# A two-layer image model on one Trainium2 core: zero rows written behind the upsampled filters, constants loaded beside the upsampling, an own order for image 0's first pass, and the convolution's input ahead of the scan constants

## The chip, the cores and the metric

The kernel runs as one program on one core of a Trainium2 chip. The core has a matrix engine (TensorE, PE in the profile; its weight loads are the row PEld), a vector engine (DVE), an activation engine (ACT), a general engine (POOL) and SyncE (SP), which here issues every DMA of the program. Each engine runs its own instructions in order and waits for the others on semaphores. The metric is the device time of one execution in microseconds. Before the change it is 26376.83 us, the median of three runs (26376.42 to 26384.82).

## The reference, cut to what matters

The input is `x`, eight images of 128x128 pixels with 96 channels, float32. There are two layers. Each adds a mixer to its input and then a small feed-forward net whose numbers are rounded to 8-bit floats.

```python
# layer 0
x_pre = soa(einsum('bhwc,mc->bhwm', ln(x), w1))     # soa(x) = scale * relu(x)**2 + bias
xf = rfft2(x_pre)                                   # 128 x 65 frequencies, 192 channels
filts = [Rh @ cw @ Rw for cw in (cw0, cw1, cw2)]    # three small filters, upsampled to 128 x 65
gctx = ln(x).mean((1, 2)); sctx = relu(bn(ln(x) @ sp_w.T)).mean((1, 2))
r = softmax((soa([gctx, sctx] @ fc1.T) @ fc2.T).reshape(b, 3, 192), 1)
x = x + irfft2(xf * (filts * r).sum(0)) @ w2.T
x = x + ffn(ln(x))
# layer 1
xi, z = split(ln(x) @ W_in.T)
u = silu(depthwise_conv3x3(xi) + conv_b)            # zero padded
y = scan(u, forward) + scan(u, backward)            # state-space recurrence over the 16384 pixels
x = x + (y * silu(z)) @ W_out.T
x = x + ffn(ln(x))
```

The weights of an image's filters (`r`) depend on means over the whole image, so an image's first pass over its pixels has to end before its filter stage starts.

## The kernel before

`tile_metaformer_kernel` (L1679 on) sets up tensors in device memory and runs four parts one after the other.

**Zero rows.** `xcd` holds the convolution's input of all images with padding rows above and below each. L1691 to L1700 clear a tile `z` on DVE and write it with 32 DMAs (L1697 one row, L1698 nine rows, each for 128 and for 64 channels of eight images), 960 KB for an image.

**Upsampling** (`upsample_filters`, L253 to L283). The small filters are loaded into a tile `cw` that DVE clears first (L261), by three DMAs (L265). 64 groups of three channels follow: 18 matrix products (L274), one ACT copy out of PSUM into one of three buffers `upt` (L282), and one DMA of 146 KB to `tall` (L283). Four PSUM tiles go round. Then its pools are closed.

**Layer 0** (`layer0`, L286). First come 21 constant loads (most in `load`, L306, with one SP issue each), then a schedule written out by hand: each step of a group of four image rows has a time in a table, a `Plan` sorts all steps by their times, and that order is the order on the engines. The times set an order only; when an instruction runs is settled by its waits. `first_steps` is an image's first pass: 32 groups, each with a load `ax` (L359), a normalisation (L92 to L115 on DVE, ACT and POOL), four transposes on PE (L364), an ACT copy `axnt` that also sums (L370), the context product (L376 on PE, L380 on ACT), two projections of two rows each (L389 on PE, relu L402 and square L409 on ACT, scaling into `img` L416 on DVE) and a POOL copy of the sums (L428). Then `gate_steps` works out the weights `r`, and `filter_steps` runs over the 64 channel groups, `token_steps` over the 32 pixel groups. The first pass of image 1 lies beside the token steps of image 0, and so on; the first pass of image 0 has nothing beside it. It is scheduled with the table `ALONE`, which is `LAST` with other times for `keep`, and with a period of 6.0 in that table's units (L882).

**Layer 1** (`scan_layer`, L902). At its start the feed-forward constants are loaded through a pool `scf`, which is closed before the work pool `scw` is opened in the same place. Then all other constants are loaded, from L934 to L998: 53 DMAs, with the DVE and ACT work on them. After that a second `Plan` runs: convolution chunks (`conv_steps`: load `xin` L1019, nine products per half chunk against diagonal matrices `cdiag` L1035, ACT eviction `pre` L1049, silu L1060, store `ud` L1067), preparation (`prepare_steps`) and the scans (`scan_steps`), which take four fifths of the time.

Outside the hand-written plans the framework orders instructions by their dependencies and the order in the text. SP's DMAs carry eight semaphores in turn: a DMA is issued only when the eighth before it has landed.

Of the kernel before, what the change touches and what calls it, by code (L numbers as in the profile page):

```python
# [9 lines left out]
F32 = mybir.dt.float32  # L10
# [242 lines left out]
def upsample_filters(tc, p, tall):  # L253

    nc = tc.nc
    with ExitStack() as ctx:
        one = ctx.enter_context(tc.tile_pool(name="up1", bufs=1))
        two = ctx.enter_context(tc.tile_pool(name="up2", bufs=3))
        psum = ctx.enter_context(tc.tile_pool(name="upp", bufs=4, space=PSUM))
        cw = one.tile([96, 32, M * 2], F32, name="cw")  # L260
        nc.vector.memset(cw, 0.0)  # L261
        rw = one.tile([96, KW], F32, name="rw")
        nc.sync.dma_start(rw, p.rwt)
        for s, src in enumerate((p.cw0, p.cw1, p.cw2)):
            nc.sync.dma_start(cw[32 * s : 32 * s + CWW[s], 0 : CWH[s], :], src)  # L265
        cwv = cw.rearrange("p h (m c) -> p h m c", c=2)
        G = 3
        for g in range(M // G):
            ps = psum.tile([96, G, 2, KW], F32, tag="up", name="up")
            for i in range(G):  # L270
                for c in range(2):
                    for s in range(NS):
                        q = slice(32 * s, 32 * s + CWW[s])
                        nc.tensor.matmul(  # L274
                            ps[32 * s : 32 * s + 32, i, c, :],
                            cwv[q, :, g * G + i, c],
                            rw[q, :],
                            start=True,
                            stop=True,
                        )  # L280
            t = two.tile([96, G, 2 * KW], F32, tag="upt", name="upt")
            nc.scalar.copy(t, ps.rearrange("p g c k -> p g (c k)"))  # L282
            nc.sync.dma_start(tall[:, g * G : (g + 1) * G, :], t)  # L283


def layer0(tc, p, tall, x2d, xcd, zsd):  # L286

    nc = tc.nc
    with ExitStack() as ctx:
        cp = ctx.enter_context(tc.tile_pool(name="l0c", bufs=1))  # L290
        gp = ctx.enter_context(tc.tile_pool(name="l0g", bufs=1))
        psum = ctx.enter_context(tc.tile_pool(name="l0p", bufs=8, space=PSUM))
# [49 lines left out]

        wk = ctx.enter_context(tc.tile_pool(name="l0w", bufs=2))

# [488 lines left out]
        ALONE = {**LAST, "keep": (-3.4, -5.3)}  # L833
# [47 lines left out]
        with tc.manual_schedule():  # L881
            at = first(0, 0.0, 6.0, ALONE, ALONE, ALONE)  # L882
            for b in range(B):
                steps = filter_steps(wk, FILTER)
                plan.pipeline(at, range(M // 3), 3.6, lambda g: steps)
                at += (M // 3 - 1) * 3.6 + 16.6
                if b < B - 1:
                    begin = first(b + 1, at, 11.6, FIRST, NEXT, LAST)
                tsteps = token_steps(b, wk, TOKEN)
                plan.pipeline(at, range(NTG), 11.6, lambda g: tsteps)  # L890
                at = begin
            plan.emit()
# [9 lines left out]
def scan_layer(tc, p, x2d, xcd, zsd, ud, yfd, dld, bcd, out):  # L902
# [11 lines left out]
    with ExitStack() as ctx:  # L914
# [8 lines left out]
        with tc.tile_pool(name="scf", bufs=1) as lp:  # L923
            ffn = Ffn(nc, cp, lp, "f1", p.f1_w1t, p.f1_b1, p.f1_w2t, p.f1_b2, ident8, mhalf)
        wk = ctx.enter_context(tc.tile_pool(name="scw", bufs=2))
        w1 = ctx.enter_context(tc.tile_pool(name="sc1", bufs=1))
        psa = ctx.enter_context(tc.tile_pool(name="scpa", bufs=2, space=PSUM))
        ps1 = ctx.enter_context(tc.tile_pool(name="scp1", bufs=1, space=PSUM))

        wo = cp.tile([128, 3, 2, C + 1], F32, name="wo")  # L930
        nc.vector.memset(wo, 0.0)
        for h in range(2):
            q = slice(64 * h, 64 * h + 64)
            nc.sync.dma_start(wo[q, :, h, 0:C], p.woutt.rearrange("(n d) c -> d n c", d=64))  # L934
            nc.vector.reduce_sum(
                wo[q, :, h, C : C + 1], wo[q, :, h, 0:C], axis=mybir.AxisListType.X
            )

        selx = cp.tile([128, 4, 128], F32, name="selx")
        nc.sync.dma_start(selx, p.selx)  # L940
        sely = cp.tile([128, 32], F32, name="sely")
        nc.sync.dma_start(sely, p.sely)

# [7 lines left out]
        dtb = cp.tile([128, 2, 2], F32, name="dtb")  # L951
        for k, parts in enumerate(kinds):
            for q, c in parts:
                nc.sync.dma_start(cwt[q, k, :], p.conv_w[c, :])
                nc.sync.dma_start(cbt[q, k : k + 1], col(p.conv_b, c.start, c.stop))
                for d in range(2):
                    lo, hi = d * M + c.start, d * M + c.stop
                    nc.sync.dma_start(dtb[q, d, k : k + 1], col(p.dt_b, lo, hi))
        at = cp.tile([128, 2, NB, NG], F32, name="at")
        nc.sync.dma_start(at, p.a_logs)  # L960
        nc.scalar.activation(at, at, AF.Exp)
        nc.vector.tensor_scalar(at, at, -1.0, None, ALU.mult)
        cdiag = cp.tile([128, 2, 9, 128], F32, name="cdiag")

        ddiag = cp.tile([128, 3, 128], F32, name="ddiag")
        dsk = cp.tile([128, 2, 3], F32, name="dsk")
        for h in range(2):
            for d in range(2):
                nc.sync.dma_start(
                    dsk[64 * h : 64 * h + 64, d, :],  # L970
                    p.ds[d * M : (d + 1) * M].rearrange("(n c) -> c n", c=64),
                )
        dsum = cp.tile([128, 3], F32, name="dsum")
        nc.vector.tensor_tensor(dsum, dsk[:, 0, :], dsk[:, 1, :], ALU.add)
        for n in range(3):
            nc.vector.tensor_scalar(ddiag[:, n, :], ident, dsum[:, n : n + 1], None, ALU.mult)
        for k in range(2):
            for j in range(9):
                nc.vector.tensor_scalar(
                    cdiag[:, k, j, :], ident, cwt[:, k, j : j + 1], None, ALU.mult  # L980
                )

        NX = 4 * NST + 2 * NR
        xpw = cp.tile([128, 2, 3, NX], F32, name="xpw")
        nc.vector.memset(xpw, 0.0)
        dtw = cp.tile([NX, 2, 3, 128], F32, name="dtw")
        nc.vector.memset(dtw, 0.0)
        for d in range(2):
            for t in range(3):
                for q, b, c in tile_parts(0, t):  # L990
                    for lo, n, at0 in (
                        (NR, NST, b * NST),
                        (NR + NST, NST, 2 * NST + b * NST),
                        (0, NR, 4 * NST + b * NR),
                    ):
                        nc.sync.dma_start(xpw[q, d, t, at0 : at0 + n], p.xpt[d, c, lo : lo + n])
                    lo = 4 * NST + b * NR
                    nc.sync.dma_start(dtw[lo : lo + NR, d, t, q], p.dtt[d, :, c])  # L998
# [653 lines left out]
        with tc.manual_schedule():  # L1652
            plan = Plan()
            plan(-300, lambda: nc.vector.memset(h0, 0.0))
            for bp in range(B // 2):
# [23 lines left out]
def kernel(ctx: ExitStack, tc: tile.TileContext, p: Params, out: bass.AP):  # L1679
# [11 lines left out]
    with tc.tile_pool(name="zero", bufs=1) as zp:  # L1691
        z = zp.tile([128, (HB + 1) * W], F32, name="z")
        nc.vector.memset(z, 0.0)
        for b in range(B):
            for c in (slice(0, 128), slice(128, M)):
                n = c.stop - c.start
                nc.sync.dma_start(xcd[b, c, 0, :], z[:n, 0:W])  # L1697
                nc.sync.dma_start(  # L1698
                    xcd[b, c, H + 1 : XROWS, :], z[:n, :].rearrange("p (h w) -> p h w", w=W)
                )  # L1700

    upsample_filters(tc, p, tall)
# [111 lines left out]
```

## Time and profile before

The profiled execution took 26377.52 us, of which the span from the first to the last instruction is 26375.7 us. Stage borders below are from the instructions in order of time.

| stage | from us | to us | what ends it |
|---|---|---|---|
| zero rows, first loads | 0.0 | 29.3 | SP issues the upsampling's first load |
| clear and load `cw` | 29.3 | 53.9 | third slice of `cw` landed |
| upsampling on PE | 53.9 | 137.3 | last L274 product |
| constants of layer 0, first `ax` | 137.3 | 152.1 | first L92 of image 0 |
| image 0, first pass | 152.1 | 373.9 | last context sum (L380) |
| its weights | 373.9 | 385.0 | first L528 of the filter stage |
| rest of layer 0 | 385.0 | 5146.0 | last ACT step of the last token group |
| constants of layer 1 | 5146.0 | 5182.9 | first L1035 |
| convolution ahead of the scans | 5182.9 | 5323.6 | first L1252 |
| scans | 5323.6 | 26375.7 | end |

| engine | busy us | share of the span |
|---|---|---|
| PE | 22322.2 | 85% |
| DVE | 25019.3 | 95% |
| ACT | 17618.2 | 67% |
| POOL | 22505.7 | 85% |

A row of instructions gives its start in us after the span's start, its length, the engine, the line, what it writes and reads, how many were merged, and in brackets how long the engine was idle before it and who ended that. "SPq" rows are DMA issues: the time is that of the issue, not of the transfer.

### The profile page before, as it was taken

Reading aid. Unit: us, or ns where it says so; the run is one execution under the profiler, and the core shown is the slowest. Engines: PE = TensorE matmul, PEld = TensorE weight load, DVE = VectorE, ACT = ScalarE, POOL = GpSimd, SP = SyncE. Lnnn points to the kernel's source line nnn. Section 1 sums busy time; section 2 is a strip of 40 time slices with the busy share of each in tenths; the row PEclk is TensorE's granted clock in tenths of the full one; section 3 lists DMA queues with packets and bytes.
Section 4 is the critical chain, followed back from the end, with each engine's and each line's share of the span. In section 5 each row is a group of like instructions: output and inputs, shape, how many; then the busy total and the mean of one; then the engine's idle time right before and its main releaser. Section 6 shows DMA issues by size and latency. Waiting matters only on the chain.

```text
span 26375.7 us, 272252 instructions
## 1 busy us (share of the span) xinstructions
PE 22322.2 (85%) x84560; PEld 8957.9 (34%) x84560; DVE 25019.3 (95%) x18514; ACT 17618.2 (67%) x31776; POOL 22505.7 (85%) x13815
## 2 busy tenths in 40 slices
PE   8999999889997777899977778998777788877777
PEld 6777777622222222222222222222222222212222
DVE  5888888699999999999999999999999999999999
ACT  5888887556666666666666666666666666656666
POOL 3666666489999999999999999999999999999998
PEclk9999999999998888999988889999888899988888
DMA  2333333344444444444444444444444444444443
GB/s 61 94 94 95 94 92 89 86 154 154 155 159 136 136 136 139 148 158 156 155 139 135 138 135 155 154 153 154 140 137 137 136 151 155 153 144 135 135 139 114
DMA packets 1887106, 3513.56 MB, mean 133 GB/s; under 512 B 564382, under 2 KB 999190, under 8 KB 1885626
## 3 DMA queue, kind: packets, MB, share of 16 engines
q1 hardware_dynamic: 1885652, 3496.14, 41.7%
q8 instruction: 672, 11.01, 0.2%
q14 instruction: 782, 6.41, 0.1%
HBM read 2739.32 MB, written 756.17 MB: 133 GB/s over the span
## 4 chain that ended last, share of the span: by engine, by line
DVE 41%; PE 18%; issue 15%; ACT 4%; POOL 3%; DVEq 0%; DMA 0%; POOLq 0%; ACTq 0%
DVE hp L1287 22%; DVE hp L1252 17%; PE pv L1035 6%; PE dub L1222 5%; PE y L1312 5%; POOL hc L1303 2%; DVE e L1139 2%; ACT da L1235 1%; PE y L1354 1%; PE pd L1116 1%; PE px L1096 0%; ACT pre L1049 0%; ACT L1061 0%; ACT L1060 0%; ACT ff_h L1543 0%
## 5 line engine op out<-in xcount | busy, mean ns | idle before, releaser
L1303 POOL TENSOR_TENSOR hc<-hp,ct 128x1024 f32<-128x1024 f32 x6144 | 14732.5, 2418 | 1175.4 <-DVE hp L1287 1048.3
L1287 DVE TENSOR_TENSOR_SCAN hp<-da,h,hp 128x1024 f32<-128x1024 f32 x6144 | 14143.0, 2338 | 207.3 <-ACT da L1235 49.0
L1312 PE MATMUL y<-hc,sely 128*32 128x512 f32 x24576 | 6959.0, 651 | 2061.1 <-POOL hc L1303 2045.0
L1235 ACT ACTIVATE da<-dlb,at 128x1024 f32<-128x1024 f32 x6144 | 6844.8, 1114 | 0.5 <-ACT h L1296 0.5
L1252 DVE TENSOR_TENSOR hp<-bt,dub 128x2048 f32<-128x2048 f32 (+1 forms) x3072 | 6558.2, 2135 | 13.4 <-PE dub L1222 12.9
L1222 PE MATMUL dub<-du,selx 128*128 128x512 f32 x6144 | 3800.0, 751 | 1332.0 <-DVE hp L1252 1331.7
L1296 ACT COPY h<-hp 128x1 f32<-128x1 f32 x6144 | 1159.1, 189 | 4769.7 <-DVE hp L1287 4753.4
L1035 PE MATMUL pv<-xin,cdiag 128*128 128x512 f32 x6912 | 3495.5, 625 | 113.8 <-ACT pre L1049 52.2
L1312 PEld LDWEIGHTS y<-hc,sely 128*32 128x32 f32 x24576 | 938.8, 112 | 6575.8 <-POOL hc L1303 4361.2
L1222 PEld LDWEIGHTS dub<-du,selx 128*128 128x128 f32 x6144 | 1286.0, 226 | 3478.7 <-issue 2164.0
L1035 PEld LDWEIGHTS pv<-xin,cdiag 128*128 128x128 f32 x6912 | 1174.5, 190 | 2466.2 <-issue 2066.4
L110 POOL TENSOR_SCALAR ln_v<-ln_v 128x4 f32<-128x4 f32 x768 | 199.9, 260 | 1288.0 <-DVE ln_v L106 1267.9
L1271 POOL TENSOR_TENSOR hp<-bt,dus 128x1024 f32<-128x1024 f32 x366 | 867.4, 2370 | 254.7 <-ACT dus L1264 204.4
L1049 ACT ACTIVATE pre<-pv,cbt 128x512 f32<-128x512 f32 x384 | 263.8, 687 | 1102.0 <-PE pv L1035 914.1
L1116 PE MATMUL pd<-bc,dtw 12*128 12x512 f32 x1536 | 913.4, 675 | 67.7 <-ACT rl L1126 47.0
L1144 POOL TENSOR_TENSOR w<-w,e 128x1024 f32<-128x1024 f32 x384 | 904.7, 2356 | 51.7 <-ACT w L1136 38.2
L111 POOL TENSOR_TENSOR ln_r<-ln_v,mhalf 128x4 f32<-128x4 f32 x768 | 885.7, 1153 | 64.0
L1154 POOL TENSOR_TENSOR du<-w,u 128x1024 f32<-128x1024 f32 x384 | 908.9, 2367 | 0.2
L1147 POOL TENSOR_TENSOR w<-w,rl 128x1024 f32<-128x1024 f32 x384 | 906.6, 2361 | 0.2
L1125 ACT ACTIVATE e<-pd,dtb 128x512 f32<-128x512 f32 x768 | 524.9, 683 | 549.5 <-PE pd L1116 532.9
L742 PE MATMUL ring<-xnt,win 96*128 96x512 f32 x1536 | 782.3, 617 | 70.8 <-ACT xnt L736 69.8
L1096 PE MATMUL px<-u,xpw 128*76 128x512 f32 x1536 | 717.2, 603 | 59.8 <-ACT ff_h L1536 57.5
(189 smaller groups left out, 32947.9 us busy)
## 6 DMA issues: line engine op xcount, KB each, us to landing
dlb<-dld SPq DMA_DIRECT2D x1536, 512.0 KB, 5.2
bt<-bcd SPq DMA_DIRECT2D x1024, 512.0 KB, 4.7
ct<-bcd SPq DMA_DIRECT2D x1024, 512.0 KB, 4.7
u<-ud SPq DMA_DIRECT2D x384, 512.0 KB, 5.0
dld<-w SPq DMA_DIRECT2D x384, 512.0 KB, 3.5
ud<-pre SPq DMA_DIRECT2D x192, 512.0 KB, 4.2
yf<-ud SPq DMA_DIRECT2D x768, 128.0 KB, 4.8
yfd<-yo SPq DMA_DIRECT2D x384, 256.0 KB, 7.1
```

Source lines behind the costliest of these rows:

```text
L1035: nc.tensor.matmul(st["pv"], cdiag[:, kind(t), j, :], st["xin"][:, r : r + HB // 2, j % 3 : j % 3 + W], start=(j == 0), stop=(j == 8),)
L1116: nc.tensor.matmul(pd, dtw[4 * NST : NX, d, t, :], k.bc[4 * NST : NX, hs], start=True, stop=True)
L1144: nc.gpsimd.tensor_tensor(st["w"], st["w"], st["e"], ALU.subtract)
L1147: nc.gpsimd.tensor_tensor(st["w"], st["w"], st["r"], ALU.add)
L1154: nc.gpsimd.tensor_tensor(k.du[t], st["w"], k.u[t], ALU.mult)
L1222: nc.tensor.matmul(blk["du"][:, hs], selx[:, blk["r"], :], k.du[blk["t"]][:, hs], start=True, stop=True,)
L1235: nc.scalar.activation(un["da"], blk["dl"], AF.Exp, scale=at[:, d, blk["kb"], j : j + 1])
L1252: nc.vector.tensor_tensor(hp[:, 0:n, :], bt[blk["b2"], j][:, 0:n, :], blk["du"].rearrange("p (o t) -> p o t", o=1).to_broadcast([128, n, TC]),
L1287: nc.vector.tensor_tensor_scan(h, da, h, un["init"], op0=ALU.mult, op1=ALU.add)
L1296: nc.scalar.copy(un["init"], un["h"][:, last : last + 1])
L1303: nc.gpsimd.tensor_tensor(un["hc"], un["h"], ct[blk["b2"], j], ALU.mult)
L1312: nc.tensor.matmul(y[q, :], sely, un["hc"][:, hs], start=False, stop=(j == NG - 1),)
```

## The change

Four edits, all ahead of the scans.

1. `upsample_filters` becomes a class. Its set-up runs at the head of `layer0`, ahead of the constant loads; half of `cw` is cleared by POOL, and `z` too. Its products run after the constant loads, and the zero rows are written one by one behind every second group's store to `tall`.
2. The constant loads of layer 0 therefore stand in SP's queue ahead of (the first 12) and behind the loads of `cw`, all ahead of the stores to `tall`. The layer's PSUM pool opens after the upsampling's is closed.
3. Image 0's first pass has a table of its own and the period 3.8. The order on PE changes from transposes, projection 0, context, projection 1 of a group to transposes of group g+1, context of g, both projections of g+1; on ACT the relus and squares of g lie around the copy `axnt` of g+1; on DVE the two `keep` of g around the sums of g+3. The POOL copy of the sums moves two groups ahead.
4. In `scan_layer` the loads of `cwt` and `cbt` and the building of `cdiag` come first, then the feed-forward loads, then two loads of `xin`; the other constants are loaded by two steps of the plan behind them.

```diff
-def upsample_filters(tc, p, tall):
...
-        nc.vector.memset(cw, 0.0)
+class Upsample:
...
+        nc.vector.memset(cw[:, 0:16], 0.0)
+        nc.gpsimd.memset(cw[:, 16:32], 0.0)
...
+        self.z = one.tile([128, (HB + 1) * W], F32, name="z")
+        nc.gpsimd.memset(self.z, 0.0)
+
+    def zero_rows(self, xcd):
+        for b in range(B):
+            for c in (slice(0, 128), slice(128, M)):
+                n = c.stop - c.start
+                self.nc.sync.dma_start(xcd[b, c, 0, :], self.z[:n, 0:W])
+                yield
+                self.nc.sync.dma_start(
+                    xcd[b, c, H + 1 : XROWS, :], self.z[:n, :].rearrange("p (h w) -> p h w", w=W)
+                )
+                yield
+
+    def run(self, tall, xcd):
+        nc, G = self.nc, 3
+        fills = self.zero_rows(xcd)
         for g in range(M // G):
...
             nc.sync.dma_start(tall[:, g * G : (g + 1) * G, :], t)
+            if g % 2 == 1:
+                next(fills, None)
...
 def layer0(tc, p, tall, x2d, xcd, zsd):
...
-        psum = ctx.enter_context(tc.tile_pool(name="l0p", bufs=8, space=PSUM))
+        up = ExitStack()
+        upsample = Upsample(up, tc, p)
...
             ffn = Ffn(nc, cp, lp, "f0", p.f0_w1t, p.f0_b1, p.f0_w2t, p.f0_b2, ident8, mhalf)
 
+        upsample.run(tall, xcd)
+        up.close()
+
         wk = ctx.enter_context(tc.tile_pool(name="l0w", bufs=2))
+        psum = ctx.enter_context(tc.tile_pool(name="l0p", bufs=8, space=PSUM))
...
-        ALONE = {**LAST, "keep": (-3.4, -5.3)}
+        ALONE = {
+            "load": -28.0,
+            "norm": (-17.00, -16.75, -15.14, -14.73, -12.58, -11.86),
+            "turn": -9.39,
+            "turned": -8.91,
+            "context": -5.52,
+            "contexts": -4.52,
+            "project": (-7.95, -6.88),
+            "relu": (-7.42, -5.25),
+            "square": (-6.37, -5.10),
+            "keep": (-5.74, -4.34),
+            "keep_sums": -14.0,
+        }
...
-            at = first(0, 0.0, 6.0, ALONE, ALONE, ALONE)
+            at = first(0, 0.0, 3.8, ALONE, ALONE, ALONE)
...
 def scan_layer(tc, p, x2d, xcd, zsd, ud, yfd, dld, bcd, out):
...
+        cwt = cp.tile([128, 2, 9], F32, name="cwt")
+        cbt = cp.tile([128, 2], F32, name="cbt")
...
+                nc.vector.tensor_scalar(
+                    cdiag[:, k, j, :], ident, cwt[:, k, j : j + 1], None, ALU.mult
+                )
         with tc.tile_pool(name="scf", bufs=1) as lp:
             ffn = Ffn(nc, cp, lp, "f1", p.f1_w1t, p.f1_b1, p.f1_w2t, p.f1_b2, ident8, mhalf)
         wk = ctx.enter_context(tc.tile_pool(name="scw", bufs=2))
...
+        def prepare_constants():
...
+        def scan_constants():
+            nc.sync.dma_start(at, p.a_logs)
+            nc.scalar.activation(at, at, AF.Exp)
...
             plan(-300, lambda: nc.vector.memset(h0, 0.0))
+            plan(UN * -2 + 20, prepare_constants)
+            plan(UN * -2 + 37, scan_constants)
...
-    with tc.tile_pool(name="zero", bufs=1) as zp:
...
-    upsample_filters(tc, p, tall)
     layer0(tc, p, tall, x2d, xcd, zsd)
```

`prepare_constants` holds the loads of `dtb`, `xpw` and `dtw` (38 DMAs), `scan_constants` those of `at`, `selx`, `sely`, `dsk` and `wo` (9 DMAs) with the DVE and ACT work on them. The numbers of groups, products and bytes are the same in both kernels.

## The prediction

> **What bounds the kernel now.** I read the page first, to see how much of the run the change can reach.
>
> ```profile
> span 26375.7 us, 272252 instructions
> PE   8999999889997777899977778998777788877777
> DVE  5888888699999999999999999999999999999999
> ```
>
> The reader is to see that from the ninth slice on (659 us each) DVE is busy nine tenths and more: the scans bound themselves there, and no edit touches their order. The change lies in the first slice, where DVE is at 5, and in the eighth, at 6, where layer 0 ends. So I left the totals and read those stretches in order of time.
>
> ```profile
> 32.02 10.30 DVE L261 MEMSET cw<- 96x12288 f32 x1 [29.98 <-DMA rw<-in_rwt_dram]
> 42.35 0.99 SPq L265 DMA_DIRECT2D cw<-in_cw_dram  x3
> 53.89 83.16 PEld L274 LDWEIGHTS up<-rw,cw 13*32 13x32 f32 x2288 [3.61 <-DMA cw<-in_cw_dram]
> 139.85 0.36 SPq L306 DMA_DIRECT2D cos<-in_cos_dram  x1
> 149.44 166.32 SPq L359 DMA_DIRECT2D ax<-in_x_dram  x28
> ```
>
> One thing follows another: zero rows to 29 us, clearing, loading `cw`, 83 us of products, constants, then the first `ax`. The first pass starts with L92 at 152.13. A group of it is this, on PE and ACT:
>
> ```profile
> 355.85 1.65 PE L389 MATMUL ring<-w,axnt 96*128 96x192 f32 x4 [0.85 <-ACT axnt L370]
> 357.43 1.94 PE L376 MATMUL ring<-axnt,spw 96*48 96x512 f32 x2
> 359.30 1.65 PE L389 MATMUL ring<-w,axnt 96*128 96x192 f32 x4
> 360.74 1.06 PE L364 MATMUL ring<-ident,axn 128*96 128x128 f32 x4
> 361.94 0.58 ACT L370 ACTIVATE axnt<-ring 96x512 f32<-96x512 f32 x1
> ```
>
> The next group starts at 362.65: the period is 6.80 us, of which PE waits 0.85 for `axnt` and works the rest. PE bounds the pass, and at half its speed: the same products elsewhere take half the time. Of the two rows, the first is from the window 150 to 384 us, the second from 600 to 5000 us (images 1 to 7); the middle number is the median in ns.
>
> ```profile
> L376 PE MATMUL ring<-axnt,spw x64: 1061/1075/1089, 160.0 to 371.9; 96*48 96x512 f32 x64
> L376 PE MATMUL ring<-axnt,spw x448: 592/593/1089, 611.2 to 4551.7; 96*48 96x512 f32 x150
> ```
>
> **1. The head, 0 to 152 us: 43 us less.** By the changed instruction lists SP issues `rw`, 12 constants, then `cw`. Thirteen issues at 0.465 us (before: `cos` at 139.85 to `win` at 145.43 is 12 in 5.58) from 0.72 put the first `cw` issue at 6.8. The clearing must be done: DVE's half is 5.15 us of the 10.30 from 1.03, to 6.2; POOL's half is taken from its memset rows, 117 ns for 10 elements and 204 for 128, hence 0.74 ns each, 4.6 us from 0.4. So the issue decides. `cw` to full flow was 42.35 to 53.90, 11.55 us; 18.4 now, and with 12 loads just ahead of it I take 19. That is 35 us earlier. Zero rows no longer stand ahead of it.
>
> [...] No row here has the two memsets together: side by side 6.2, one after the other 1.0 + 5.15 + 4.6 = 10.8, 4 us later. [...]
>
> The products are the same 2304 in 83.4 us (53.90 to 137.3). Beside the `tall` stores now go the 32 zero writes:
>
> ```profile
> 0.00:30.00 30.00, 0.00 (x0) 0.00 (x0) 1.02 (x1) 1.28 (x1) 0.19 (x4) 1.00 0.93 273
> 54.00:138.00 84.00, 83.30 (x2288) 83.06 (x2288) 0.00 (x0) 30.69 (x64) 0.00 (x0) 1.00 0.41 116
> ```
>
> The last two columns are the DMA share and GB/s. 0.93 of 30 us and 0.41 of 84 make 62 us of full DMA work for an 84 us stretch: three quarters. A 576 KB write takes 2.1 us at 273 GB/s, so a `tall` store behind it lands in 4.3 instead of its 2.2; its buffer is wanted after three groups of 1.30 us less the 0.48 us copy, 3.4. ACT is late by 0.9, which four PSUM tiles (3.4 us of slack) hide from PE. I charge 1 us; without the cover it is 16 large writes by 0.9 = 14.
>
> After the last product: before, 2.5 us to the last landing, 9.6 of constant issues, 2.7 for `ax`: 14.8. Now the `ax` load waits for the last `tall` landing alone: 2.5 + 2.7 = 5.2, 9.5 less. The constants, behind `cw` in SP's queue, land during the products; the ring of eight holds `bmean` and the rest until the last `cw` slice lands, so the first `tall` store issues about 1 us late, under the three buffers. Sum 35 - 1 + 9.5 = 43.5.
>
> **2. Image 0's first pass: 92 us less.** In the new order PE does transposes of g+1, context of g, projections of g+1; `axnt` of g+1 (0.62 us) now hides under the context product (1.87 from start to start). At the slow speed a group is 0.95 + 1.8 + 2.7 (eight passes, the first of the block 0.16 longer) = 5.5 us without a wait. At the fast one about 593/1075 of it, 3.0, and ACT becomes the bound. ACT from start to start, rows of the same stretch: `r` to `q` 0.53, `q` to the next 0.43 (361.51 to 361.94), `axnt` with its accumulator 0.57, `sj` with its own 0.76 (0.67 + 0.09), `ln_q` 0.43; with two `r` and two `q`: 3.6 to 3.7. DVE has 3.2 busy, POOL 1.7; the DVE-POOL chain of a group runs two groups ahead. I take 3.65.
>
> Which speed? [...] The page's granted clock is 1.00 in both speeds, so durations must tell. The row: 220 us with PE at work 5.95 of 6.80 left it slow. [...] The nearest row is the start of the filter stage, the first work without a wait:
>
> ```profile
> 386.77 1.64 PE L561 MATMUL ring<-fw,fo 128*128 128x130 f32 x6 [7.57 <-DVE fo L551]
> 393.10 0.83 PE L561 MATMUL ring<-fw,fo 128*128 128x130 f32 x6
> ```
>
> After 6.3 us without a gap the same six passes take half. [...] Slow throughout is the other end. [...] Sum: 31 periods by 6.80 - 3.65 = 98, less 4 for the slow start and 2 for a longer fill: 92. Slow throughout: 31 by 1.3 - 1 = 39. The weights' 11 us chain after the last context sum stays.
>
> **3. The handoff: 23 us less.** Before, `xin` is issued behind 53 constants:
>
> ```profile
> 5178.05 1.09 SPq L1019 DMA_DIRECT2D xin<-xcd  x2
> 5182.90 10.74 PE L1035 MATMUL pv<-xin,cdiag 128*128 128x512 f32 x18 [38.26 <-DMA xin<-xcd]
> ```
>
> Now five small loads and four feed-forward loads follow the last store (5147.1), the last issued at 5151.2. The `xin` load has a new wait: its space is that of the feed-forward staging tiles, so `f_b2f` must land (3.1 us, from 5148.23 to its cast at 5151.31) and be cast: 5154.8. Behind it in SP's queue stand the 38 constants of the next step, which nobody wants before the `px` product 64 us later. Plus the 4.85 us from `xin` issue to PE: 5159.7 against 5182.9. `cdiag` (two blocks of 1.85) is ready by 5153. The 38 issues take until 5177, the first `ud` store is due 22.7 us after the first product, 5182: 5 us of cover. The nine of the later step (5.3 us) lie between two `ud` stores 18 us apart; the Exp of `at` is 0.24 us on ACT. From the first product to the first scan the chain of waits is PE and ACT alone, so the shift reaches the end. If the wait for `f_b2f` weren't there: 27; if SP's order slipped by its cover: 20.
>
> **Sum.** 43.5 + 92 + 23 = 158.5 off the profiled execution's 26377.5: **26219 us**, 0.6% less. That execution stands 0.7 us over the median of the runs.
>
> **Rivals.**
> - Gate stays shut in the first pass: 43.5 + 39 + 23 = 105.5, **26272 us**. For it: 220 us at nearly full work were not enough. Against: the filter stage's start. 0.12.
> - Zero writes hold the upsampling, PE being stopped by each large one: 14 to 25 us dearer, **26240 us**. For it: ACT already waits for `tall` stores before (7.9 us). Against: the DMA share of 0.74. 0.09.
> - Slower: the scans, 21052 us long, start at another place of the clock gate's pattern. Some `dub` products (L1222, 1536 blocks of four passes) run slow, 3.5 us instead of 1.98. From about 100 more slow blocks on the path (100 by 1.6 = 160) the gain is gone; 150 would give **26460 us**. For it: `dub` is 5% of the chain that ended last. Against: three runs, whose phases nothing aligns, lie within 8.4 us. 0.03.
> - The main case: 0.76.
>
> The measurement tells 0.2%, 53 us, from no change. Faster 0.96, same 0.01, slower 0.03. The range of 26200 to 26280 takes the 4 us of the clearing, a 3.55 us period and 27 at the handoff on one side, the shut gate on the other.
>
> **What would show it.** First 13-row product by 20 us, first L92 by 109; L376's median in the first pass near 593 with a period of 3.6 to 3.7 from the fourth group on; `ACT` without idle rows there; weights done some 138 us after the first L92; first L1035 14 us after the last ACT step of layer 0; scans as long as before within 10 us. A period of 5.5 with medians of 1075 would mean the shut gate, PE idle in the upsampling the crowded DMA queue.

## The result, and the profile after

The changed kernel takes **26212.69 us** (median of four runs, 26202.5 to 26216.56) against 26380.41 us (four runs) of the kernel before in the same round: ratio 0.9936, interval 0.9919 to 0.9953. The profiled execution took 26211.62 us. The forecast was 26219.

First the page of the changed kernel, the rows that were shown of before:

```profile
span 26209.8 us, 272243 instructions
PE   9999999899997777889877778889777788977777
DVE  7888888699999999999999999999999999999999
```

DVE's first digit went from 5 to 7, PE's from 8 to 9: the first slice holds less waiting. From the ninth slice on DVE is as full as before: the scans still bound themselves. Stage by stage, with the borders of the table of before:

| stage | before, us | after, us | gain | forecast |
|---|---|---|---|---|
| head, to the first L92 | 152.1 | 114.3 | 37.8 | 43.5 |
| image 0's first pass, to the last context sum | 221.8 | 118.1 | 103.7 | 92 |
| its weights | 11.1 | 9.7 | 1.4 | 0 |
| rest of layer 0 | 4761.0 | 4765.5 | -4.5 | 0 |
| handoff, last ACT step to first convolution product | 36.9 | 14.6 | 22.3 | 23 |
| convolution ahead of the scans | 140.7 | 142.9 | -2.2 | 0 |
| scans | 21052.1 | 21044.8 | 7.3 | 0 |

The gains add up to the 165.9 us between the two spans. Two of the rows are no effect of the change: in the ten profiled kernels below without a probe, before and after among them, the rest of layer 0 took 4757.0 to 4768.8 us and the scans 21044.7 to 21055.0, whatever was edited elsewhere.

**The head**, from instructions of the changed kernel in order of time (start, length, engine):

```profile
0.72 5.21 POOL L263 MEMSET cw<- 96x6144 f32 x1 [0.29 <-POOLq L1838]
...
2.07 5.18 DVE L262 MEMSET cw<- 96x6144 f32 x1 [2.07 <-issue]
...
7.27 1.02 SPq L267 DMA_DIRECT2D cw<-in_cw_dram  x3
...
19.29 0.98 PE L293 MATMUL up<-rw,cw 13*32 13x65 f32 x21 [3.84 <-DMA cw<-in_cw_dram]
...
111.34 9.35 SPq L387 DMA_DIRECT2D ax<-in_x_dram  x6
114.31 0.55 DVE L92 TENSOR_REDUCE ln_s<-ax 128x4 f32<-128x384 f32 x1 [88.77 <-DMA ax<-in_x_dram]
```

The two clearings overlap for 3.9 us, and DVE's half takes 5.18 us beside POOL's, half of the 10.30 us that the whole took alone: they do not shut each other out. DVE began at 2.07, where the forecast had 1.03, so its half ended at 7.25 and not the issues but the clearing let the `cw` load go at 7.27. The products flow from 19.29, 35 us earlier, as forecast. (Their count in the profile, 2304, is passes, two for each of 1152 products.) But they last until 106.96, 87.7 us instead of 83.4, and the first L92 comes 7.35 us later instead of 5.2. ACT's waits, total, times and longest, show why:

```profile
ACT upt L301 <- DMA tall<-upt: 55.1, 27, 3.7
```

Before, it was 7.9 us in 7 waits, the longest 1.7.

**The first pass**, again in order of time:

```profile
222.15 1.57 PE L417 MATMUL ring<-w,axnt 96*128 96x192 f32 x8 [0.35 <-ACT axnt L398]
...
223.63 0.64 PE L392 MATMUL ring<-ident,axn 128*96 128x128 f32 x4
...
224.21 1.06 PE L404 MATMUL ring<-axnt,spw 96*48 96x512 f32 x2
...
224.88 0.58 ACT L398 ACTIVATE axnt<-ring 96x512 f32<-96x512 f32 x1
...
225.61 1.57 PE L417 MATMUL ring<-w,axnt 96*128 96x192 f32 x8 [0.34 <-ACT axnt L398]
```

Eight passes of the projections take 1.57 us; four took 1.65 before. The period is 3.46 us, and PE waits only for `axnt`. ACT is the engine that is full, 105.99 of 107 us (busy time in us and instructions of PE, PEld, DVE, ACT, POOL, then granted clock, DMA share, GB/s):

```profile
125.00:232.00 107.00, 96.09 (x432) 56.29 (x430) 86.15 (x179) 105.99 (x279) 51.24 (x87) 1.00 0.21 53
```

Minimum, median and maximum of the context product in this pass, in ns:

```profile
L404 PE MATMUL ring<-axnt,spw x64: 592/612/649, 124.4 to 230.6; 96*48 96x512 f32 x64
```

Before it was 1061/1075/1089. PE runs at full speed from the first context product on.

**The handoff**:

```profile
5013.84 0.48 SPq L142 DMA_DIRECT2D f_b2f<-in_f_b_dram  x1
...
5017.09 0.21 DVE L144 CAST f_b<-f_b2f 128x96 fp8e5<-128x96 f32 x1 [1.19 <-DMA f_b2f<-in_f_b_dram]
5017.33 0.21 DVE L146 CAST f_b<-f_b 128x96 f32<-128x96 fp8e5 x1
5017.57 1.06 SPq L1065 DMA_DIRECT2D xin<-xcd  x2
...
5022.14 9.89 PE L1081 MATMUL pv<-xin,cdiag 128*128 128x512 f32 x18 [15.94 <-DMA xin<-xcd]
...
5064.35 0.54 DVE L1038 MEMSET wo<- 128x582 f32 x1
5064.92 1.25 SPq L1041 DMA_DIRECT2D wo<-in_woutt_dram  x2
5066.27 0.54 SPq L1113 DMA_DIRECT2D ud<-pre  x1
...
5070.23 0.69 ACT L1095 ACTIVATE pre<-pv,cbt 128x512 f32<-128x512 f32 x1 [7.04 <-DMA ud<-pre]
5070.98 9.39 PE L1081 MATMUL pv<-xin,cdiag 128*128 128x512 f32 x18 [3.64 <-ACT pre L1095]
```

The `xin` load is issued 0.03 us after the last cast of the feed-forward staging. The last five lines hold what the forecast missed: SP stands at the `wo` load until `wo` is cleared; the `ud` store that wrote behind it is late, ACT waits 7 us for the buffer, PE 3.6.

### The profile page after: what moved, and what is told of

The parts are those of the page before. It is cut to its first block, busy times and chain, and to the rows that moved or that the text cites. A ratio compares the mean times of both kernels' runs of the same rounds, so it can differ in the third digit from the quotient of the medians.

```text
span 26209.8 us, 272243 instructions
## 1 busy us (share of the span) xinstructions
PE 22077.0 (84%) x84560; PEld 8860.1 (34%) x84560; DVE 25009.4 (95%) x18513; ACT 17596.9 (67%) x31774; POOL 22513.3 (86%) x13817
## 4 chain that ended last, share of the span: by engine, by line
DVE 41%; PE 17%; issue 16%; ACT 5%; POOL 3%; DMA 0%; DVEq 0%; POOLq 0%; SPq 0%; ACTq 0%
DVE hp L1333 22%; DVE hp L1298 17%; PE pv L1081 6%; PE y L1358 5%; PE dub L1268 4%; POOL hc L1349 2%; DVE e L1185 2%; ACT da L1281 2%; PE po L1492 1%; PE y L1400 1%; PE px L1142 1%; ACT ff_h L1589 0%; ACT ln_q L1519 0%; PE pd L1162 0%; ACT pre L1095 0%
## 5 line engine op out<-in xcount | busy, mean ns | idle before, releaser
L1268 PE MATMUL dub<-du,selx 128*128 128x512 f32 x6144 | 3686.2, 731 | 1385.5 <-DVE hp L1298 1385.3
L770 PE MATMUL ring<-xnt,win 96*128 96x512 f32 x1536 | 778.5, 615 | 69.1 <-ACT xnt L764 68.1
```

The source lines that it names most:

```text
L1268: nc.tensor.matmul(blk["du"][:, hs], selx[:, blk["r"], :], k.du[blk["t"]][:, hs], start=True, stop=True,)
```

## The experiments

The theory under test had four parts: the new order opens PE's clock in the first pass; the zero writes crowd the upsampling; the handoff is bound by the staging's cast; the convolution loses what SP loses at `wo`. The first pass is two thirds of the gain, so it was taken first.

### The old order in the new place

```diff
-        ALONE = {"load": -28.0, "norm": (-17.00, ...
+        ALONE = {**LAST, "keep": (-3.4, -5.3)}
-            at = first(0, 0.0, 3.8, ALONE, ALONE, ALONE)
+            at = first(0, 0.0, 6.0, ALONE, ALONE, ALONE)
```

> The changed kernel with the old table and the old period for image 0's first pass; the head and the handoff stay changed. Theory (the order opens the clock: the 0.85 us in which PE waits for axnt in each group keep it at the slow speed, wherever the pass stands): the pass falls back to a period of 6.8 us, the context product's median to 1075 ns, first L92 to last context sum from 118 back to some 222 us, the whole run to about 26213 + 104 = 26317 us. Rival (the new place opens it: PE comes out of the upsampling after 12 us of rest instead of 23 us, or the DMA queues are emptier): median near 593 ns, pass well under 180 us, run within 40 us of 26213.

Median 26316.01 us (nine runs), ratio to before 0.9977 (0.9967 to 0.9987). The pass takes 221.8 us, as before to the tenth. The context product from 113 us to 340 us:

```profile
L404 PE MATMUL ring<-axnt,spw x64: 1061/1075/1089, 121.4 to 333.3; 96*48 96x512 f32 x64
```

So the 103.7 us come with the new order; the earlier start and the emptier queues give the old order nothing.

### The old order with its gap filled, by a large and by a small product

In both, one product more per group of image 0, between the transposes and the first projection; nothing reads it.

```diff
+                if b == 0:
+                    spare = ring([128, 384])
+                    nc.tensor.matmul(
+                        spare, ident, st["axn"].rearrange("p h c -> p (h c)")[:, 0:384],
+                        start=True, stop=True,
+                    )
```

The second takes 32 rows of `ident` and of `axn` instead of 128.

> The old order as in the run before, plus one product of 128 rows by 384 columns per group on PE between the transposes and the first projection, there where PE waits for axnt; nothing reads what it writes. Theory (gaps on PE keep the clock shut): with the wait filled the clock opens, the context product's median goes to about 593 ns, the period to 4 to 5 us though PE has more to do, and the pass to 130 to 160 us. Rival (the gain of the new order is the overlap itself and the clock comes along for another reason): products stay at 1075 ns, the period stays at 6.8 to 7.2 us, the pass at 220 us or above.

> As the run with the filling product in the old order, but the product has 32 rows instead of 128 (same 384 columns, same place, so the same time on PE). Theory (streamed columns times rows in a window open the clock): the wait is filled as before, but a window gains at most 0.05 of the full measure; the old order's densest window, 0.74, holds four transposes and hardly any of the wait, so it stays below what opens the clock, and the pass stays slow: context product 1075 ns, period 6.8 to 7.4 us, pass 220 to 240 us, the run near 26320 us. Rival (PE at work without a pause is what counts): it opens as with 128 rows, pass near 158 us, run near 26255 us.

128 rows: median 26255.16 us, pass 157.8 us. 32 rows: one run of 26336.33 us, pass 242.8 us, a little beyond the expected end. The context products, 128 rows first:

```profile
L410 PE MATMUL ring<-axnt,spw x64: 592/612/799, 122.7 to 270.9; 96*48 96x512 f32 x64
```

```profile
L410 PE MATMUL ring<-axnt,spw x64: 1061/1075/1089, 124.5 to 356.6; 96*48 96x512 f32 x64
```

The same place filled for the same length: with 128 rows the old order runs at full speed, although PE has more to do; with 32 rows it stays slow (context product 1075 ns), at a period of 7.46 us in which PE never waits. Two things follow. In the old order the clock alone is worth at least 64 of the 103.7 us (221.8 less 157.8), in spite of the added product. The other 40 come with what else the new order does, which no run takes apart: at full speed the filled old order waits 0.6 us a group for DVE's `axn`. And filling time was not enough: with the same time filled, 128 rows opened the clock and 32 rows did not.

### Two probes of the clock

Blocks of like products between the upsampling and the first pass, each after a rest of about 14 us. Nothing reads their results. From the first probe:

```diff
+            def block(rows, cols, n, gap):
+                for k in range(n):
+                    nc.tensor.matmul(acc[0:cols, :], ident[0:rows, 0:cols], mov[0:rows, :], ...)
+                    if gap and k % gap == gap - 1:
+                        nc.scalar.copy(out[0:cols, :], acc[0:cols, :])
```

> The changed kernel with a probe put between the upsampling and the first pass: blocks of 40 like products of 512 columns, each block after a rest of some 14 us in which ACT alone works: 128 rows by 128 columns, 96 by 128, 64 by 128, 32 by 128, 96 by 48, 128 by 32; then 60 products of 128 by 128 and of 96 by 128 with a wait for an ACT copy (about 0.9 us) after each six. Nothing reads the results. Theory (the clock opens on the mean activity of a window, counted by rows, not on time at work alone): 128 rows without gaps change from about 1.07 to about 0.6 us per product within 7 us; 64 and 32 rows stay at 1.07 to the end of their 40; 96 rows without gaps open, later or as fast as 128; with gaps 128 rows open and 96 rows do not. Rival (one busy window is enough, whatever the rows): all blocks without gaps open within 7 us, 32 rows too, and the two blocks with gaps behave alike.

> A second probe in the same place, after rests of 14 us: 30 products of 512 columns with 72, 80 and 88 rows; the products of 14 groups of the first pass (four transposes, projection, context, projection) without a wait; the same 14 groups with the ACT copy that the old order waits for; 40 products of 128 rows with a wait for ACT after each two; 30 with a wait after each one. Theory (what opens the clock is streamed columns times rows in a window; before, 0.60 of the full measure on the mean and 0.68 in the stretch without a wait; threshold between 0.68 and 0.75): 72 and 80 rows (0.56, 0.63) stay at 0.85 us per pass to the end, 88 rows (0.69) stand on the edge, the groups without a wait (0.74) open, those with it stay shut, 128 rows open after each two (0.79) and stay shut after each one (0.65). Rival (the wait alone decides, rows only between 64 and 96): 72, 80 and 88 rows open within 7 us, and both 128-row patterns with waits do the same as the groups with a wait.

PE's rows of the first probe; the count is passes, two per product:

```profile
126.50 37.18 PE L380 MATMUL acc<-mov,ident 128*128 128x512 f32 x80 [14.86 <-ACT pout L391]
178.59 36.74 PE L380 MATMUL acc<-mov,ident 96*128 96x512 f32 x80 [14.91 <-ACT pout L387]
230.24 68.63 PE L380 MATMUL acc<-mov,ident 64*128 64x512 f32 x80 [14.91 <-ACT pout L387]
313.79 68.63 PE L380 MATMUL acc<-mov,ident 32*128 32x512 f32 x80 [14.91 <-ACT pout L387]
...
448.61 36.47 PE L380 MATMUL acc<-mov,ident 128*32 128x512 f32 x80 [14.75 <-ACT pout L387]
...
578.29 7.38 PE L380 MATMUL acc<-mov,ident 96*128 96x512 f32 x12 [15.53 <-ACT pout L387]
586.41 5.42 PE L380 MATMUL acc<-mov,ident 96*128 96x512 f32 x12 [0.73 <-ACT pout L385]
```

The granted clock, third column from the end, for the blocks of 128, 64 and 32 rows:

```profile
132.00:163.00 31.00, 31.00 (x73) 13.68 (x72) 0.00 (x0) 0.00 (x0) 0.00 (x0) 1.00 0.00 0
231.00:298.00 67.00, 67.00 (x80) 25.97 (x78) 0.00 (x0) 0.00 (x0) 0.00 (x0) 0.50 0.00 0
314.00:382.00 68.00, 68.00 (x80) 26.26 (x80) 0.00 (x0) 0.00 (x0) 0.00 (x0) 0.50 0.00 0
```

And PE's rows of the second probe:

```profile
132.28 25.92 PE L386 MATMUL acc<-mov,ident 72*128 72x512 f32 x60
...
174.00 51.57 PE L386 MATMUL acc<-mov,ident 80*128 80x512 f32 x60 [10.40 <-ACT pout L382]
240.48 51.57 PE L386 MATMUL acc<-mov,ident 88*128 88x512 f32 x60 [14.91 <-ACT pout L382]
...
315.14 2.93 PE L393 MATMUL acc<-mov 96*128 96x192 f32 x8
318.00 1.94 PE L409 MATMUL acc<-mov 96*48 96x512 f32 x2
...
547.00 2.07 PE L386 MATMUL acc<-mov,ident 128*128 128x512 f32 x2 [15.53 <-ACT pout L382]
549.75 2.08 PE L386 MATMUL acc<-mov,ident 128*128 128x512 f32 x2 [0.68 <-ACT pout L388]
```

Eighty passes in 68.6 us are 0.85 us each, from the first to the last: the blocks of 64 and 32 rows never open the clock, though PE never waits in them. By the clock record of this run, 128 and 96 rows open it after 5.2 and 4.4 us. With 32 columns written instead of 128 the block of 128 rows takes 36.47 us, against 37.18: their number made no difference to the opening here. Of 88 rows not one of 60 passes is fast: they take 51.57 us, 0.86 each. ("Open" stands for full speed, a granted clock of 1.00, "shut" for half of it, 0.50.)

A measure that sorts most of these is columns streamed (1.67 ns each at the slow speed, 0.853 us for 512) times the share of 128 rows, over the time. A group of the first pass streams 512 columns of 128 rows and 2560 of 96 rows: 4.05 us of full measure. Hence:

| pattern | measure | clock |
|---|---|---|
| 64 rows, no wait | 0.50 | shut for 68 us |
| old order, gap filled with 32 rows (4.37 in 7.46 us) | 0.59 | shut |
| old order (4.05 in 6.80 us) | 0.60 | shut |
| 128 rows, ACT wait after each product (1.71 in 2.75 us) | 0.62 | shut |
| 96 rows in short products, no wait (3.20 in 4.73 us) | 0.68 | shut for 66 us |
| 88 rows, no wait | 0.69 | shut for 52 us |
| new order at the slow speed (4.05 in 5.59 us, start of the pass in the last kernel below) | 0.72 | opens |
| 96 rows of 512 columns, no wait | 0.75 | opens |

So in these runs the steady patterns of 0.69 and less left the clock shut for as long as they ran, and those of 0.72 and more opened it. A mean over a loop is not the whole of it. The last expectation for the groups with ACT's copy failed: at a mean of 0.66 they opened the clock 43 us after the start of their block. Why, no run shows.

The clock records of the kernels before and after say a little more. In each of the two traces all changes of the granted clock (1524 records before, 1356 after) lie on one grid of 3.41 us. Summed over the steps of that grid, which is an estimate from the starts of the passes, good to about 0.03, the measure swings between 0.45 and 0.74 in the groups of the first pass before, and the clock stays shut. The step ahead of the opening at 392.8 us, in the filter stage of before, held 0.90; the one ahead of the opening at 124.5 us, in the first pass after, 0.77. The estimate covers these stretches alone.

Staying open took less than opening. The 72 rows, expected to stay slow, ran their 60 passes at full speed, 25.92 us or 0.43 each: 15 us of transposes of 128 rows had been put ahead of them and had opened the clock. The 80 and 88 rows, which started with the clock shut, stayed slow. And 96 rows with gaps did not stay shut, as expected of them: the first six products run 7.4 us without a wait and open it, and the gaps of 0.73 us that follow each six products of 5.42 us do not shut it again. As expected, 128 rows opened it with a wait after each two products, 3.1 us in, and not with a wait after each one (2.07 us for each to the end).

(The program differs from the expectation in the groups of the second probe. The transposes took two passes each instead of one. All those of the block "without a wait" and the first ones of the block with the copy were put ahead of the 72 rows or just behind them; so the block "without a wait" became the row of 0.68.)

### The zero writes elsewhere, or more buffers

```diff
-            if g % 2 == 1:
-                next(fills, None)
+                    for k in range(4 * B):
+                        plan(at + 7.2 * k + 1.0, lambda: next(fills))
```

> The changed kernel with the 32 zero writes moved out of the upsampling into the filter stage of image 0 (one every second channel group; the source is one cleared row read nine times, for want of space). Theory (the zero writes crowd the stores to tall, and ACT, held by its three buffers, stops PE): first to last L293 product 83.5 to 84.0 us instead of 87.7, ACT's wait for tall stores from 55 back to about 8 us, last product to first L92 5.2 to 5.8 us instead of 7.35, so first L92 near 109 us instead of 114.3; filter stage of image 0 longer by no more than 3 us. Rival (the 12 constants or the stores themselves slow the upsampling): it stays at 87 us or more.

```diff
-        self.two = ctx.enter_context(tc.tile_pool(name="up2", bufs=3))
+        self.two = ctx.enter_context(tc.tile_pool(name="up2", bufs=8))
```

> The changed kernel with eight instead of three upt buffers; the zero writes stay where they are. Theory (the zero writes only delay single stores; the DMA engines have room, 62 us of full work in 84): deeper buffers take up the delays, the upsampling from first to last product of 13 rows goes from 87.7 to 83.5 to 84.5 us, ACT's wait for tall stores from 55 us to under 10; the tail to the first L92 stays at 7 to 9 us since the last stores still queue behind zero writes. Rival (the transfers themselves bound the stretch): still 87 us or more, whatever the buffers.

ACT's waits, of the first and then of the second kernel:

```profile
ACT upt L300 <- PE up L292: 45.6, 34, 18.8
ACT upt L300 <- DMA tall<-upt: 25.8, 15, 2.9
```

```profile
ACT upt L301 <- DMA xcd<-z: 11.5, 14, 0.8
ACT upt L301 <- DMA tall<-upt: 3.3, 4, 0.8
```

Without the zero writes the products run from 19.2 to 102.6, 83.4 us, and the first L92 comes 5.8 us later, at 108.5. The first term of the sum is restored, the second (5.2) all but 0.6 us. ACT still waits 25.8 us, not 8, yet PE loses nothing: these waits stay under the slack. With eight buffers the products take 84.1 us (19.9 to 104.0), but the tail stays at 7.3. So the delay is of single stores and buffers cure it; the tail is shortened only by moving the writes. Total times were 26204.98 and 26208.6 us, one run each. In their new place the writes cost nothing that shows: image 0's filter stage, from its first to its 64th L528 step (by the lines of before), takes 208.9 us, and 208.7 in both of the last kernels below, which also have the writes there; without them it takes 208.5 to 209.2 in the six other kernels with the new head.

### The handoff

```diff
+        with tc.tile_pool(name="scf", bufs=1) as lp:
+            ffn = Ffn(nc, cp, lp, "f1", ...
         cwt = cp.tile([128, 2, 9], F32, name="cwt")
...
-        with tc.tile_pool(name="scf", bufs=1) as lp:
-            ffn = Ffn(nc, cp, lp, "f1", ...
...
         def prepare_constants():
+            nc.vector.memset(wo, 0.0)
...
-            nc.vector.memset(wo, 0.0)
```

> The changed kernel with two things moved at the handoff: the feed-forward constants are loaded ahead of cwt and cbt, and wo is cleared with xpw and dtw, one step earlier. Theory for the first: xin waits for the cast of f_b2f, so the step from the last ACT work of layer 0 to the first convolution product falls from 14.6 to 11 to 12 us. Rival: xin waits for something else (its own landing, the stores of xcd), it stays at 14 or more. Theory for the second: in the changed kernel SP stands 1.9 us or more at the wo load until wo is cleared behind the Exp of at and its table load, so the second ud store is late, ACT waits 7 us for the pre buffer and PE 3.6 us; without that the convolution ahead of the scans goes from 143 to 138.5 to 140 us. Rival: the store itself takes that long, 143 stays.

One run of 26206.99 us. From the last ACT step to the first product 11.5 us, and the convolution takes 139.4 us. In the two later kernels with this edit it is 11.7 and 11.2, 138.6 and 139.6; in the six with the changed kernel's handoff 14.2 to 14.6, and 142.9 to 146.1. PE's waits between 5020 us and the first scan, changed kernel and then this one:

```profile
PE pv L1081 <- ACT pre L1095: 6.9, 5, 3.6
```

```profile
PE pv L1081 <- ACT pre L1095: 4.1, 5, 0.9
```

The long wait is gone, and with it the slow start behind it. Both theories held.

### Two faster upsamplings

Both with the three cures above. The first lays the small filters out as blocks on a diagonal and makes one product of three; the second keeps three and takes each over 32 rows.

```diff
-                    for s in range(NS):
-                        q = slice(32 * s, 32 * s + CWW[s])
-                        nc.tensor.matmul(
-                            ps[32 * s : 32 * s + 32, i, c, :],
-                            self.cw[q, :, g * G + i, c],
-                            self.rw[q, :],
...
+                    m = g * G + i
+                    nc.tensor.matmul(
+                        ps[:, i, c, :],
+                        self.cw[m // self.N % 4][:, :, 2 * (m % self.N) + c],
+                        self.rw,
...
```

```diff
-                        q = slice(32 * s, 32 * s + CWW[s])
+                        q = slice(32 * s, 32 * s + 32)
```

> The changed kernel with the zero writes in the filter stage of image 0, eight upt buffers, both moves at the handoff, and the three bands of a filter upsampled in one product: cw is laid out as three blocks on the diagonal of 96 rows by 96 columns (four tiles of 24 channels in turn), so 768 products of 96 rows take the place of 2304 in the three bands. Theory (a product's time goes by its streamed columns, not its rows): a group of three channels costs PE 0.65 us at the slow speed instead of 1.30, and the upsampling is bound by its stores, 9.6 MB at about 280 GB/s, 35 to 45 us; the first L92 comes at 58 to 68 us instead of 114, and with 7 us at the handoff the run takes 26145 to 26165 us. Rival (the row bands run side by side already and one large product takes as long as three): no gain in the upsampling, first L92 at 105 us or later, the run near 26197 us.

> The changed kernel with the zero writes in the filter stage of image 0, eight upt buffers, both moves at the handoff, and the upsampling's products taken over all 32 rows of each band instead of 9, 4 and 13 (the added rows are zero on both sides; cw and rw are cleared there already), three band products side by side as before. Theory (the clock counts streamed columns times rows, and rows of products running side by side add up): three bands of 32 rows make 96 rows streaming without a pause, 0.75 of the full measure, as much as the 96-row block of the first probe, which opened within 5 us; the upsampling then runs at the full speed, 0.65 us a group instead of 1.30, and its stores bound it at 38 to 48 us; first L92 at 66 to 76 us instead of 114.3, the run at 26145 to 26165 us. Rival (bands do not add up, a product counts its own 32 rows): the upsampling stays at 83.5 us, first L92 at 108 to 109 us, the run at 26194 to 26200 us.

The first is slower than the changed kernel: 26231.23 us (four runs), first L92 at 139.4 us. A group takes 1.97 us, from one ACT copy to the next, instead of 1.30; a pass is 164 ns where three passes in the bands take 108 ns together, which is just the 65 columns at 1.67 ns. The bands run side by side already. What the other 56 ns of the large product are stays open. That it pays for its weight loads is not shown: in the first probe the 64-row passes, with a weight load of 0.33 us beside each, start 0.853 us apart, the time of their 512 columns alone.

The second is the fastest kernel here: **26188.08 us** (five runs), ratio to before 0.9927 (0.9913 to 0.9941). Its clock opens 11 us after the bands flow, while bands of 9, 4 and 13 rows left it shut to the end. So in this run the rows of bands side by side added up, and rows that hold zeros counted: 32 rows alone left it shut for 68.6 us in the first probe. The gain is still short of the expectation: the products take 68.1 us (19.3 to 87.4), not 38 to 48, and the first L92 comes at 93.2. PE's rows, the granted clock in two stretches as above, and a row of the DMA queues from 34 to 57 us (transfers, MB, share of the 16 engines):

```profile
38.26 2.65 PE L292 MATMUL up<-rw,cw 32*32 32x65 f32 x128 [1.35 <-issue]
41.71 2.65 PE L292 MATMUL up<-rw,cw 32*32 32x65 f32 x128 [0.80 <-issue]
```

```profile
31.00:57.00 26.00, 19.09 (x935) 18.17 (x932) 0.00 (x0) 12.52 (x26) 0.00 (x0) 1.00 0.54 160
58.00:64.70 6.70, 6.70 (x188) 6.49 (x184) 0.00 (x0) 2.64 (x6) 0.00 (x0) 0.50 0.45 127
```

```profile
q8 instruction: 6, 0.10, 1.8%
```

Three bands now take 57 ns from start to start instead of 108, but after each 128 passes, 256 instructions with their weight loads, PE stands still for 0.8 to 1.6 us, and the wait is put down to nothing. No other engine or store holds it. What fits is the supply of instructions: from 34 to 57 us there are six such pauses and six transfers of 16384 bytes on the queue named `instruction`, and each of the pauses that were timed, twelve up to 86 us, ends 1.3 to 1.5 us after such a transfer has landed. At the slow speed 128 passes take 4.6 us and no pause shows. No run changes that supply, so this is the author's reading and not shown by experiment. After the longest pause the clock, too, shut for 6.8 us, from 57.9 on.

## Why the prediction was right or wrong

The time is right within 6.3 us of the median and 7.4 of the profiled execution. That it is so close is luck, since errors cancel: the head 5.7 us dearer, the first pass and the weights 13.1 us cheaper, handoff and convolution 2.9 dearer, and 2.8 from the two stages that vary from run to run.

- **First product at 19.** Right: 19.29. The clearing side by side held (3.9 us of overlap), and the 4 us that the range kept for it were not needed. That "the issue decides" was wrong by a little: DVE's clearing ended last, at 7.25, when the issues were done at 6.82; and POOL's half took 5.21 us, not 4.6.
- **"I charge 1 us" for the zero writes.** This step failed. The sum put a delay of 0.9 us on each large write and let four PSUM tiles hide it. The stores came late in bunches, waits up to 3.7 us against the 3.4 of slack, and PE lost 3.3 us more than charged; the tail grew by 2.1 us, of which moving the writes gives 1.5 back. The rival that crowds the upsampling had the mechanism, and less than half its price: 4.3 us of products and 2.1 of tail, where it gave 14 to 25.
- **Period 3.65, bound by ACT.** The bound was right, the size was 3.46. The term is `r`: 0.53 from start to start was taken twice, as `r` to the `q` that waits for it. In the new order one `r` is followed by `axnt` (224.51 to 224.88, 0.37) and the other by its `q` at 0.50; 31 periods make 6 us of it. The other 6 are the slow start, taken at 4 us, and the fill, taken at 2. No run shows either: 31 times 6.80 - 3.46 is 103.5 us, the pass is 103.7 shorter. PE was slow from its first transposes at 118.88 to the opening at 124.5, little more than one group, and the last groups, with no normalisation beside them, run in 3.04 us (225.61 to 228.65 from projection to projection) and less.
- **"After 6.3 us without a gap the same six passes take half."** From this one row the forecast estimated the full speed for the new order, which at the slow speed has no wait either. The result was right, but the row is only half of it. The old order was not shut by its wait alone: with the wait filled by 32 rows PE never waits, and the context product stays at 1075 ns; 88 rows without any wait stay at 0.86 us a pass for 51.57 us. What fits the runs is that in the new order, with the wait hidden, the same columns and rows fall into 5.59 us instead of 6.80, a measure of 0.72 instead of 0.60.
- **Weights after the pass unchanged.** 1.4 us cheaper. The products of `fc` take 2.20 us in both kernels; but before, the last projection ran until 374.56, past the last context sum at 373.9, and DVE scaled its result ahead of the weights' steps. In the new order that projection is done before.
- **Handoff 23 us, 3.6 of it lost to `f_b2f`.** Right: 22.3, and moving the staging gives 3.1 back.
- **"The nine of the later step (5.3 us) lie between two `ud` stores 18 us apart; the Exp of `at` is 0.24 us on ACT."** This failed. ACT loads a table of 1.28 us ahead of it, the Exp waits behind the next chunk's silu, DVE clears `wo` only after it, and SP, in order, holds the `ud` store for the `wo` load. The issues were counted, what they wait for was not: 3.5 us by the runs without it.
- **Scans as long as before within 10 us.** Right, 7.3 us apart, and no more than chance; the slower rival did not come up.

## What to carry to other kernels

When PE is slow in a loop that keeps it busy, count its streamed columns times rows before looking for gaps. Here reordering to hide a wait, or one free product of 128 rows, took the context product from 1075 to 612 ns, and a filling of 32 rows left it at 1075. Once open, the clock bore gaps of 0.73 us after each 5.42 us of products of 96 rows. When DMA issues are moved into a queue that others share, write down for each what it waits for, and put what clears its target ahead of the move. Put bulk writes that nobody needs soon where no ring of few buffers passes through the same queues: moved away, they gave the upsampling 4.3 us back (87.7 to 83.4).

## What the runs showed that was not expected

- Adding zero rows to the upsampling's products cost no time: three bands take 108 ns at the slow speed with 4 to 13 rows and with 32. With 32 the clock opened 11 us in, and then they take 57 ns.
- Work without a wait did not always open the clock: steady patterns of 0.69 of the full measure and less left it shut for 51 us and more, those of 0.72 and 0.75 opened it. Groups at a mean of 0.66 opened it all the same, 43 us in.
- The upsampling's products in different bands of 32 rows run side by side: three passes of 65 columns take 108 ns together at the slow speed, and a single one over 96 rows and 96 columns takes 164.
- At full speed the upsampling's small products pause for 0.8 to 1.6 us after each 128 passes, in step with transfers of 16384 bytes on the queue `instruction`.
- The granted clock of the profile reads 1.00 in the first pass before and after, at both speeds. It is not blind to the difference: the trace's first clock record is at 392.8 us before and at 124.5 after, and ahead of the first record the column reads 1.00 whatever the speed. From there on it follows, as the 0.50 of the 64-row block shows.
